# Grouped logits issued two pairs at a time over all eight PSUM banks, in a four-layer cross-attention kernel

## The chip, the cores and the metric

The kernel runs on one NeuronCore of one Trainium2 chip. The metric is device microseconds of one execution: the median of three runs before the change is 3410.82 us (3410.70 to 3411.05). Engines are called PE (TensorE matmul), PEld (its weight loads), DVE (VectorE), ACT (ScalarE), POOL (GpSimd) and SP (SyncE, which issues DMAs).

## The reference

Four cross-attention layers run one after the other on a state `x` of 4 batches, 512 queries and 256 channels, all in float32, with a context of 1024 keys and 512 channels. Layers 0, 2 and 3 ("masked") have 16 heads of 64 and add a bias to the logits of a few key columns; layer 1 ("grouped") normalises `x` first and has 16 heads of 16 that share 4 key/value heads:

```python
# masked layers 0, 2, 3
logits = einsum('bhqd,bhkd->bhqk', x @ Wq, ctx @ Wk) * 64 ** -0.5 + col_bias
x = softmax(logits) @ (ctx @ Wv) @ Wo + bo + x
# grouped layer 1
xn = rmsnorm(x, norm_w)
scores = einsum('btgrd,bsgd->bgrts', xn @ wq, ctx @ wk) * 16 ** -0.5
x = x + softmax(scores) @ (ctx @ wv) @ wo
```

The softmax subtracts a maximum before the exponential, so the maximum of the logits is computed too.

## The kernel before, in words

**Units and steps.** A unit is a pair of heads of a masked layer, or four heads' worth of a grouped layer (`u` from 0 to 7 in each layer and batch; `g.h` is `u % 2`). `order()` writes out by hand which masked unit `g` and which grouped unit go together. The main loop runs over these steps. In a step, `g` is the masked unit whose logits are made, `g1` the masked unit of the step before, which is attended, `lam` the grouped unit that is attended, and `coming` the grouped unit of the next step, whose logits are made already now. There are 32 steps with a `coming`; in 28 of them there is also a `lam` (in the first of each batch there is none).

**One step on PE**, in order: `scores(g)` (L873, with two bfloat16 bias matmuls, L879), `attend(g1)` (L906), then a list `fill` of pieces of projections: the queries of the next unit (L770), output projections (L1112), and either the keys of the next two masked units (`k_part`, L556: a "key step") or the values of two (`v_pair`, L609: a "value step"). Two successive pieces of keys or of values fill one PSUM bank, which ACT copies out (L561, L616) after the second. After roughly 9.5 us of fill by a hand-written estimate (8.0 in value steps) come the sums of `g1` (L1078) and `attend_grouped` (L906 with 128x32 tiles), and from 12 us on the four calls of `logits_pair` for `coming` (L846), spread between the remaining fill pieces by due times.

**A pair** is two tiles of 128 keys by 1024 (two heads by 512 queries). It is eight PE instructions in tiles of 32 rows, four of which run at once. Each tile takes two PSUM banks. ACT copies it to SBUF (L852), DVE takes its block maxima (`block_max`, L930), and after the last of eight tiles `max_quarters` and `max_everywhere` (L946 to L970) make the maximum of the unit. In the next step POOL subtracts it from the eight tiles (`subtract`, L976), ACT takes the exponentials (L984), and then `attend_grouped` can run.

**After the grouped attention**, `keep_even` (ACT, L916) copies one half of the result from its PSUM bank and `keep_odd` (DVE, L920) adds the other half. For units with `g.h == 1`, which are attended in key steps, `turn_grouped` then normalises through the same bank (DVE, L1033 to L1039).

**PSUM.** `Place` hands out the 8 banks: two-bank places go to even pairs, one-bank places in these steps to banks 4 to 7, the longest free first. The matmul that takes a bank waits for whoever read it last. All orders on the engines are those in which the program issues; there is no other scheduler.

Of the kernel before, what the change touches and what calls it, by code (L numbers as in the profile page):

```python
# [17 lines left out]
B, S, C = 4, 512, 256  # L18
# [62 lines left out]
def kernel(ctx: ExitStack, tc: tile.TileContext, a: dict, out: bass.AP):  # L81
# [17 lines left out]
    returns = [0]  # L99

    tabled = [False]

    class Place:
        def __init__(self, width=2, last=2, among=(4, 5, 6, 7)):
            free = given_back
            if width == 2:
                whole = [n for n in range(0, 8, 2) if n in free and n + 1 in free]
                if tabled[0]:
                    whole = [n for n in whole if n <= last] or whole
                at = min(whole, key=lambda n: max(free[n], free[n + 1]))  # L110
            elif tabled[0] and any(n in free for n in among):
                at = min((n for n in among if n in free), key=lambda n: free[n])
            else:
                at = min(free, key=lambda n: free[n] + (2 if n ^ 1 in free else 0))
            self.banks = range(at, at + width)
            for n in self.banks:
                del free[n]
            self.ap = ps_all[:, at : at + width, :].rearrange("p n q -> p (n q)")
# [642 lines left out]
    def project_q(g):  # L761
        if g.n in first_queries:
            g.qt = x_all[:, g.n // 2, g.n % 2, :]
        else:
            g.qt = t_([P, S], "qt", f"qt_{g.name}", bufs=2)
        x = xs[g.l, g.b]
        w = Place(1)
        m = w.ap
        for k in range(KC):
            nc.tensor.matmul(m, lhsT=g.wq[:, k, :], rhs=x[:, k, :], start=(k == 0), stop=(k == KC - 1))  # L770
        if g.last:
            drop_state(g.l, g.b)

        def evacuate():
            nc.scalar.mul(g.qt, m, 0.125)
            w.back()

        return evacuate
# [59 lines left out]
        return evacuate  # L838


    def logits_pair(g, i):
        ws = [Place(), Place()]
        for odd in range(2):
            for j in range(2):
                rows = slice(64 * odd + 32 * j, 64 * odd + 32 * (j + 1))
                nc.tensor.matmul(  # L846
                    ws[odd].ap[:, j * S : (j + 1) * S], lhsT=g.kt[rows, i * P : (i + 1) * P],
                    rhs=g.qt[rows, :], start=True, stop=True,
                )
        for odd, w in enumerate(ws):  # L850
            t = 2 * i + odd
            nc.scalar.copy(g.st[t], w.ap)  # L852
            if tabled[0]:
                w.back()
                block_max(g, t)
            elif t == 0:
                g.mx_place = w
            else:
                w.back()
                top = g.mx_place.ap  # L860
                nc.vector.tensor_tensor(top, top, g.st[t], ALU.max)
# [56 lines left out]
    def keep_odd(g):  # L918
        half = gq[g.b, "o"][64 * g.h : 64 * (g.h + 1), :]
        nc.vector.tensor_tensor(half, half, g.po[64:128, :], ALU.add)  # L920
        if g.h == 0:
            g.place.back()

# [11 lines left out]
    def max_quarters(g):  # L937
        other = t_([64, 32], "other", f"other_max_{g.name}")
        g.every = t_([P, 2 * S // 32, 1], "every", f"every_{g.name}")
        if tabled[0] and g.masked:  # L940
            g.mb_place = w = Place()
        else:
            w = Place(1)
        quarter, half = w.ap[:, 0:32], w.ap[0:64, 32:64]
        if tabled[0]:
            nc.vector.tensor_reduce(quarter, tops.rearrange("p t b -> p b t"), AX.X, ALU.max)  # L946
        else:
            over_quarter(quarter, g.mx_place.ap, ALU.max)
            g.mx_place.back()
        nc.vector.tensor_copy(other, quarter[64:128, :])  # L950
        nc.vector.tensor_tensor(half, quarter[0:64, :], other, ALU.max)
        for h in range(2):
            nc.vector.tensor_copy(
                other[32 * h : 32 * (h + 1), :], half[32 * (1 - h) : 32 * (2 - h), :]
            )
        for h in range(2):
            nc.vector.tensor_tensor(
                g.every[64 * h : 64 * (h + 1), :, 0], half, other, ALU.max
            )
        if not (tabled[0] and g.masked):  # L960
            w.back()
# [61 lines left out]
        nc.gpsimd.tensor_tensor(g.acc, g.st[0] if t == 1 else g.acc, g.st[t], ALU.add)  # L1023

    def turn_grouped(g):
        normalise_grouped(g, g.place.ap)
        g.place.back()

    def normalise_grouped(g, m):

        o = gq[g.b, "o"]
        short = t_([P, S // 32, 1], "short", f"short_{g.name}")
        nc.vector.transpose(m, o)  # L1033
        nc.vector.reciprocal(short, m.rearrange("p (c r) -> p c r", r=32)[:, :, 16:17])
        nc.vector.transpose(
            m.rearrange("p (c r) -> p c r", r=32), short.to_broadcast([P, S // 32, 32])
        )
        g.ot = o
        nc.vector.tensor_tensor(o, o, m, ALU.mult)  # L1039
        if g.u % 4 == 1:  # L1040
            nc.sync.dma_start(out=o_kept, in_=o)
        else:
            for i in range(4):
                nc.sync.dma_start(
                    out=o[32 * i + 16 : 32 * (i + 1), :], in_=o_kept[32 * i : 32 * i + 16, :]
                )
# [241 lines left out]
    for n in range(len(steps) + 2):  # L1288
        g, lam = at(n)
        follows, coming = at(n + 1)  # L1290
# [5 lines left out]
        kk = []  # L1296
# [71 lines left out]
        def pair(i):  # L1368
            if i == 0:
                pass_events(STAY)  # L1370
                while late:
                    late.pop(0)()
                take_set(coming)
            logits_pair(coming, i)
            if by_ones and events:
                events.pop(0)[2]()
            if i == NT // 2 - 1:
                max_quarters(coming)
                max_everywhere(coming)
# [66 lines left out]
        of_queries = []  # L1446
        if follows and follows.n not in first_queries and not comes_late(follows, n):
            of_queries.append((1.7, lambda: project_q(follows)))
        if fast_k:
            of_keys = fast_keys(*kk)  # L1450
            if fresh:
                of_keys[1:4] = of_keys[3:4] + of_keys[1:3]
            fill = of_keys[:2] + fill + of_keys[2:4] + of_queries + of_keys[4:]
        elif fast_v:
            of_values = fast_values(g)
            if fresh:
                of_values[1:4] = of_values[3:4] + of_values[1:3]
                fill = of_values[:2] + fill + of_grouped + of_values[2:4] + of_queries + of_values[4:]
                of_grouped = []
            else:  # L1460
                fill = of_values[:2] + fill + of_queries + of_values[2:]
        else:
            fill += of_queries
            if kk:
                fill += keys(*kk)
        of_values = values(g) if g and g.n % 2 == 0 and not fast_v else []
        before = 2 if by_ones else 4
        fill += of_values[:before] + of_grouped + of_values[before:]
        if lam:

            def attend_grouped():
                while any(of is lam for _, of, _ in events):
                    events.pop(0)[2]()
                lam.v = head(lam).v
                place_out(lam)
                attend(lam)
                give_set(lam)
                late.append(lambda: keep_odd(lam))
                if lam.h == 1:
                    late.append(lambda: turn_grouped(lam))  # L1480
                return lambda: keep_even(lam)

            total, where = 0.0, 0
            while where < len(fill) and total < (8.0 if by_ones and of_values else 9.5):
                total += fill[where][0]
                where += 1
            fill.insert(where, (3.6, attend_grouped))
            if by_ones:
                fill.insert(where, (1.0, lambda: late.insert(0, sums_beside(g1))))
        elif by_ones:  # L1490
            fill.insert(2, (1.0, lambda: late.insert(0, sums_beside(g1))))
# [27 lines left out]
            fill.append((0.9, by_products))  # L1519
        now = 0.0  # L1520
        for us, w in fill:
            while pairs and pairs[0][0] <= now:
                pair(pairs.pop(0)[1])
                now += 1.0
                pairs = [(max(at, now + 1.6), i) for at, i in pairs]
            done = w()
            now += us
            if callable(done):
                pass_events(now)
                done()  # L1530
        while pairs:
            pair(pairs.pop(0)[1])
        behind_exponentials()
        if lam and lam.u % 4 == 3:
            ready.append(lam)
# [32 lines left out]
```

## Time and profile before

| what | value |
|---|---|
| median of three runs | 3410.82 us |
| profiled execution | 3411.3 us, of which span 3409.5 us |
| PE busy | 3396.9 us (100%), 15520 instructions |
| DVE, ACT, POOL busy | 2956.4 us (87%), 2348.4 us (69%), 2596.1 us (76%) |
| granted PE clock | 1.00 |
| L846 (pairs of grouped logits) | 1024 PE instructions, 160.0 us busy |
| L852 (their copies) | 256 on ACT, 1.02 us each |
| L976, L1023 (POOL subtractions, running sums) | 256 of 2.38 us, 668 of 2.37 us |

Of each execution 1.8 us lie outside the span. A PE that is busy all the time is not one that works all the time: ends of matmuls are modelled, and a short wait between two kinds of matmul doesn't show as idle time. Starts are measured, so what a group of matmuls costs is read from its start to the start of the next group.

### The profile page before, as it was taken

How to read it: one execution, taken by the hardware profiler on the slowest of the kernel's cores; microseconds unless marked ns; L12 is line 12 of the kernel's file. 1: busy time of each engine (PE TensorE's matmuls, PEld its weight loads, DVE VectorE, ACT ScalarE, POOL GpSimd, SP SyncE). 2: the span in 40 equal slices, each digit the busy share in tenths (PEclk: the TensorE clock that was granted, in tenths of full speed). 3: DMA queues.
4: the chain of work that ended last, by engine and by line, in shares of the span. 5: the costliest groups of instructions: out<-in, count | busy, mean ns of one | idle time of the engine just before them, and what ended most of it. 6: DMA issues, size and time to landing. Idle time of an engine off the chain costs nothing.

```text
span 3409.5 us, 42702 instructions
## 1 busy us (share of the span) xinstructions
PE 3396.9 (100%) x15520; PEld 1654.2 (49%) x15520; DVE 2956.4 (87%) x3872; ACT 2348.4 (69%) x2729; POOL 2596.1 (76%) x1337
## 2 busy tenths in 40 slices
PE   9999999999999999999999999999999999999999
PEld 5555444444444444445455454554444445454554
DVE  7888899988999889988888889888899988889887
ACT  5666688776787768876666666666678776666665
POOL 5888588875888768888668768677588888769775
PEclk9999999999999999999999999999999999999999
DMA  3232111011101120011001110011111101011100
GB/s 109 64 115 85 58 36 52 30 48 38 55 27 30 48 62 30 27 30 55 19 28 53 35 48 30 28 53 56 38 30 52 36 21 53 28 45 52 35 30 10
DMA packets 147733, 151.69 MB, mean 44 GB/s; under 512 B 23608, under 2 KB 125496, under 8 KB 147012
## 3 DMA queue, kind: packets, MB, share of 16 engines
q1 hardware_dynamic: 144958, 140.58, 13.2%
q0 software_dynamic: 2560, 8.39, 0.9%
q8 instruction: 123, 2.02, 0.3%
q14 instruction: 86, 0.70, 0.1%
q10 hardware_dynamic: 6, 0.00, 0.0%
HBM read 132.15 MB, written 15.73 MB: 43 GB/s over the span
## 4 chain that ended last, share of the span: by engine, by line
PE 92%; DVE 5%; ACT 1%; issue 1%; POOL 0%; DMA 0%; DVEq 0%; ACTq 0%; POOLq 0%
PE ps L906 21%; PE ps L669 18%; PE ps L873 18%; PE ps L556 9%; PE ps L609 9%; PE ps L1112 5%; PE ps L770 5%; PE ps L846 4%; DVE ps L890 2%; DVE st L978 1%; PE ps L1078 1%; PE ps L571 1%; ACT st L883 1%; PE ps L879 1%; PE ps L785 0%
## 5 line engine op out<-in xcount | busy, mean ns | idle before, releaser
L1023 POOL TENSOR_TENSOR st<-st 128x1024 f32<-128x1024 f32 x668 | 1581.7, 2368 | 557.1 <-ACT st L984 512.6
L984 ACT ACTIVATE st<-st 128x1024 f32<-128x1024 f32 x1024 | 1042.3, 1060 | 226.8 <-POOL st L976 117.7
L978 DVE TENSOR_TENSOR st<-st,ps 128x1024 f32<-128x1024 f32 x768 | 884.2, 1214 | 3.3
L906 PE MATMUL ps<-st,v 128*64 128x512 f32 (+1 forms) x4064 | 789.8, 595 | 0.0
L976 POOL TENSOR_TENSOR st<-st 128x1024 f32<-128x1024 f32 x256 | 597.8, 2379 | 212.0 <-DVE st L970 106.2
L883 ACT COPY st<-ps 128x1024 f32<-128x1024 f32 x768 | 713.3, 1053 | 55.6 <-PE ps L879 55.4
L890 DVE TENSOR_TENSOR ps<-ps,st 128x1024 f32<-128x1024 f32 x420 | 517.8, 1233 | 210.2 <-ACT st L883 172.1
L930 DVE TRANSPOSE_TENSOR_REDUCE tops<-st 128x32 f32<-128x1024 f32 x544 | 628.3, 1211 | 69.2 <-ACT st L852 64.5
L873 PE MATMUL ps<-qt,kt 64*128 64x512 f32 x3008 | 687.3, 596 | 0.0
L906 PEld LDWEIGHTS ps<-st,v 128*64 128x64 f32 (+1 forms) x4064 | 239.9, 130 | 535.0 <-issue 443.6
L873 PEld LDWEIGHTS ps<-qt,kt 64*128 64x128 f32 x3008 | 280.9, 186 | 345.0 <-ACT st L883 147.5
L609 PE MATMUL ps<-wv,ctx 128*128 128x256 f32 x1344 | 312.1, 385 | 1.1 <-ACT ctx L432 1.1
L669 PE MATMUL ps<-st 128*128 128x128 f32 (+1 forms) x1620 | 308.8, 339 | 2.3 <-ACT ps L692 2.1
L556 PE MATMUL ps<-ctx,wk 128*128 128x512 f32 x672 | 310.9, 604 | 0.0
L609 PEld LDWEIGHTS ps<-wv,ctx 128*128 128x128 f32 x1344 | 250.5, 190 | 92.1 <-issue 54.8
L852 ACT COPY st<-ps 128x1024 f32<-128x1024 f32 x256 | 247.0, 1018 | 62.5 <-PE ps L846 59.0
L669 PEld LDWEIGHTS ps<-st 128*128 128x128 f32 x1620 | 214.6, 192 | 94.2 <-issue 86.7
L684 ACT COPY st<-ps 128x512 f32<-128x512 f32 x45 | 26.3, 585 | 339.2 <-PE ps L669 339.2
L556 PEld LDWEIGHTS ps<-ctx,wk 128*128 128x128 f32 x672 | 121.9, 190 | 180.5 <-issue 163.4
L770 PE MATMUL ps<-x,wq 128*128 128x512 f32 x376 | 180.6, 603 | 2.0 <-ACT x L393 1.1
L1112 PE MATMUL ps<-ot,wo 128*128 128x512 f32 x380 | 173.2, 599 | 0.0
L846 PE MATMUL ps<-qt,kt 32*128 32x512 f32 x1024 | 160.0, 640 | 0.0
(202 smaller groups left out, 2961.6 us busy)
## 6 DMA issues: line engine op xcount, KB each, us to landing
wv<-in_L_xattn_Wv_dram SPq DMA_DIRECT2D x48, 512.0 KB
ctx<-kept SPq DMA_DIRECT2D x24, 1024.0 KB
wk<-in_L_xattn_Wk_dram SPq DMA_DIRECT2D x47, 512.0 KB
wo<-in_L_xattn_Wo_dram SPq DMA_DIRECT2D x96, 128.0 KB
wq<-in_L_xattn_Wq_dram SPq DMA_DIRECT2D x94, 128.0 KB
st<-kept SPq DMA_DIRECT2D x4, 2048.0 KB
qt<-q SPq DMA_DIRECT2D x64, 128.0 KB
kept<-st SPq DMA_DIRECT2D x12, 512.0 KB
```

The source lines that it names most:

```text
L556: nc.tensor.matmul(m, lhsT=g.w["k"][:, k, :], rhs=ctx_half[g.b, n][:, k, :], start=(k == 0), stop=(k == KT - 1),)
L609: nc.tensor.matmul(m[:, half * 2 * P : (half + 1) * 2 * P], lhsT=ctx_half[g.b, t // 4][:, k, t % 4 * P : (t % 4 + 1) * P], rhs=g.w["v2"][: ...
L669: nc.tensor.matmul(m if is_keys else m[:, q], lhsT=right[:, k, :] if is_keys else left_[:, k, q], rhs=left_[:, k, :] if is_keys else right ...
L873: nc.tensor.matmul(m[:, j * S : (j + 1) * S], lhsT=g.kt[g.rows[j], keys], rhs=g.qt[g.rows[j], :], start=True, stop=t > 0,)
L883: nc.scalar.copy(g.st[t], m)
L890: nc.vector.tensor_tensor(top, top, g.st[t], ALU.max)
L906: nc.tensor.matmul(g.po[at, :], lhsT=g.v[:, t, rows], rhs=g.st[t][:, j * S : (j + 1) * S], start=(t == first), stop=(t == last),)
L930: nc.vector.tensor_reduce(out_, of.rearrange("p (b x) -> p b x", x=32), AX.X, op, apply_transpose=True)
L976: nc.gpsimd.tensor_tensor(g.st[t], g.st[t], g.mb, ALU.subtract)
L978: nc.vector.tensor_tensor(g.st[t], g.st[t], g.mb, ALU.subtract)
L984: nc.scalar.activation(st, st, AF.Exp)
L1023: nc.gpsimd.tensor_tensor(g.acc, g.st[0] if t == 1 else g.acc, g.st[t], ALU.add)
```

## The change: what it does

In steps that have both a `lam` and a `coming`, the four pairs are no longer spread by due times. Two of them are put directly after the grouped attention, then two pieces of keys or values, then the other two, then the rest. The eight tiles get fixed banks: the pairs use (0,1)+(2,3), (4,5)+(6,7), (2,3)+(4,5), (6,7)+(0,1). The pieces after each double pair are sent to banks 0 and 2 (`hinted`). So that a bank's two pieces stay together, the grouped attention moves one piece later where an odd number of them had come before it. `turn_grouped` works in SBUF (`g.mx`), and the bank of the grouped attention is given back right after `keep_odd`. `max_quarters` of a grouped unit uses bank 7. The one masked exponential that waits among the pairs comes after the second pair instead of the first.

```diff
-        def __init__(self, width=2, last=2, among=(4, 5, 6, 7)):
+        def __init__(self, width=2, last=2, among=(4, 5, 6, 7), at=None):
             free = given_back
-            if width == 2:
+            if at is not None or width == 1 and hinted:
+                at = hinted.pop(0) if at is None else at
+            elif width == 2:
...
-    def logits_pair(g, i):
-        ws = [Place(), Place()]
+    PAIR_BANKS = ((0, 2), (4, 6), (2, 4), (6, 0))
+
+    def logits_pair(g, i, fixed):
+        ws = [Place(at=PAIR_BANKS[i][odd] if fixed else None) for odd in range(2)]
...
         nc.vector.tensor_tensor(half, half, g.po[64:128, :], ALU.add)
-        if g.h == 0:
-            g.place.back()
+        g.place.back()
...
-            w = Place(1)
+            w = Place(1, among=(7,))
...
     def turn_grouped(g):
-        normalise_grouped(g, g.place.ap)
-        g.place.back()
+        normalise_grouped(g, g.mx[:, 0:S])
...
-            logits_pair(coming, i)
-            if by_ones and events:
+            logits_pair(coming, i, bool(lam))
+            if by_ones and events and i == (1 if lam else 0):
                 events.pop(0)[2]()
...
-            while where < len(fill) and total < (8.0 if by_ones and of_values else 9.5):
+            enough = 8.0 if coming and of_values else 9.5
+            while where < len(fill) and total < enough:
                 total += fill[where][0]
                 where += 1
+            if coming:
+                where += sum(each in of_values + of_keys for each in fill[:where]) % 2
+
+                def two_pairs(bank):
+                    hinted.clear()
+                    pair(pairs.pop(0)[1])
+                    pair(pairs.pop(0)[1])
+                    hinted.extend(range(bank, bank + 2))
+
+                fill.insert(where + 2, (2.0, lambda: two_pairs(2)))
+                fill.insert(where, (2.0, lambda: two_pairs(0)))
             fill.insert(where, (3.6, attend_grouped))
...
-            while pairs and pairs[0][0] <= now:
+            while pairs and not lam and pairs[0][0] <= now:
```

## The prediction

> **What bounds the kernel now.** I read the page first, then the timelines of PE, ACT, DVE and POOL over two neighbouring steps (a key step whose first pair starts at 906.73 and a value step whose first pair starts at 948.57), then the instructions of single lines. Busy times and the chain that ended last:
>
> ```profile
> PE 3396.9 (100%) x15520; PEld 1654.2 (49%) x15520; DVE 2956.4 (87%) x3872; ACT 2348.4 (69%) x2729; POOL 2596.1 (76%) x1337
> ...
> PE 92%; DVE 5%; ACT 1%; issue 1%; POOL 0%; DMA 0%; DVEq 0%; ACTq 0%; POOLq 0%
> ```
>
> PE sets the end everywhere, so only what changes the distance between starts on PE counts. PE's timeline of the key step:
>
> ```profile
> 903.16 3.64 PE L906 MATMUL ps<-st,v 128*32 128x512 f32 x32
> 906.73 1.14 PE L846 MATMUL ps<-qt,kt 32*128 32x512 f32 x8
> 907.80 1.99 PE L556 MATMUL ps<-ctx,wk 128*128 128x512 f32 x4
> 909.72 1.34 PE L846 MATMUL ps<-qt,kt 32*128 32x512 f32 x8
> 910.99 1.98 PE L556 MATMUL ps<-ctx,wk 128*128 128x512 f32 x4
> 912.90 1.41 PE L846 MATMUL ps<-qt,kt 32*128 32x512 f32 x8
> 914.25 1.98 PE L556 MATMUL ps<-ctx,wk 128*128 128x512 f32 x4
> 916.16 1.14 PE L846 MATMUL ps<-qt,kt 32*128 32x512 f32 x8
> 917.23 3.70 PE L556 MATMUL ps<-ctx,wk 128*128 128x512 f32 x8
> 920.86 1.13 PE L873 MATMUL ps<-qt,kt 64*128 64x512 f32 x4
> ```
>
> Four key matmuls take 1.92 us from start to start (907.80 to 909.72), eight take 3.63 (917.23 to 920.86): four more cost 1.71, 0.43 each, so each group pays 0.21 for coming after another tile shape. A pair is two rounds of 0.43 and takes 1.07: again 0.21. The second and third pair take 1.27 and 1.35, 0.20 and 0.28 more; they wait for a bank. And what follows the grouped attention off PE, in the value step, from ACT's, DVE's and POOL's timelines:
>
> ```profile
> 924.22 18.69 POOL L976 TENSOR_TENSOR st<-st 128x1024 f32<-128x1024 f32 x8 [6.28 <-DVE st L970]
> ```
> ```profile
> 938.25 2.01 ACT L984 ACTIVATE st<-st 128x1024 f32<-128x1024 f32 x2 [0.47 <-POOL st L976]
> 940.60 2.00 ACT L984 ACTIVATE st<-st 128x1024 f32<-128x1024 f32 x2 [0.34 <-POOL st L976]
> 942.51 0.57 ACT L616 COPY v<-ps 128x512 f32<-128x512 f32 x1
> 942.97 3.90 ACT L984 ACTIVATE st<-st 128x1024 f32<-128x1024 f32 x4
> 946.77 0.57 ACT L616 COPY v<-ps 128x512 f32<-128x512 f32 x1
> 947.24 2.01 ACT L984 ACTIVATE st<-st 128x1024 f32<-128x1024 f32 x2
> 949.14 0.57 ACT L916 COPY o<-ps 64x512 f32<-64x512 f32 x1
> 949.78 1.93 ACT L852 COPY st<-ps 128x1024 f32<-128x1024 f32 x2
> ```
> ```profile
> 949.74 0.69 DVE L920 TENSOR_TENSOR o<-o,ps 64x512 f32<-64x512 f32 x1 [1.74 <-ACT o L916]
> ```
>
> Read the brackets: from 940.60 ACT is never idle, and it began there because POOL's subtraction had just come. So keep_even (L916, 949.14) comes 24.92 after POOL's first subtraction, by a queue and not by PE, whose attention ended at 948.57. The list of who waited for keep_odd (L920) is empty today. That is what the change alters.
>
> **The gain.** G is the start of a step's first pair. A key step takes 14.13 from G to the next scores; one key piece (1.71) moves ahead of G, so 12.42 is to be compared. New, without waits: two double pairs of 1.07 + 0.86 = 1.93 and two fills of 3.63, 11.12: 1.30 saved (two switches to pairs and two back, 0.84, and 0.48 of bank waits, rounded). A value step takes 12.37 (948.57 to 960.94) and would take 2 x 1.93 + 2 x 3.65 = 11.16: 1.21 saved. All 28 steps would give 28 x 1.26 = 35 us.
>
> **New wait 1: bank 7.** The built program of the changed kernel puts the grouped attention in bank 7 in all these steps, and the last matmul of the second pair, which writes bank 7, waits for keep_odd. keep_even starts 0.14 after G when ACT is free (0.57 in the value step above), takes 0.58, keep_odd follows 0.03 later and takes 0.69: 1.30 in all. Semaphore to matmul takes 0.05 (an L852 copy ends at 909.88, the pair's second half starts at 909.93). Today a half that starts at 909.94 lets the next group begin at 910.99: 1.05. So the double pair lasts (keep_even's delay after G) + 1.30 + 0.05 + 1.05 = delay + 2.40; with a delay of 0.14 that is 2.54 instead of 1.93. Behind that wait stand the fill, the second double pair and the next scores.
>
> **New wait 2: bank 2.** The fill after the second double pair goes to bank 2, which holds that double pair's first tile. Its copy starts 1.23 after the pairs do (917.39 after 916.16) and takes 1.01; with 0.05 the fill starts at 2.29, not 1.93: 0.36 lost in every step. The first fill's bank 0 has the same wait, hidden under wait 1. The two pieces of the first fill lie in bank 0, which the fourth pair needs 0.96 after its double pair starts; their copy ends 0.69 after (916.27 + 0.58 against 916.16): no loss. The exponential moved behind the second pair goes 4.9 to 5.9 after G, in front of that copy at 6.3: nothing, but if keep_even came over 2 us late it would delay it.
>
> **New wait 3: the loop.** keep_even's delay is itself changed. In a key step DVE ends the last block maximum 14.07 after G today (920.81). New: keep_odd ends at 1.44, turn_grouped (2.5, taken unchanged in SBUF) at 3.98, eight maxima at 1.13 end at 13.06; by copies, the second double pair starts at 2.54 + 3.63 = 6.17, its first copy ends at 8.41 and four maxima follow to 13.06. Both say 13.06. Then 3.41 to POOL's first subtraction (920.81 to 924.22) and 24.92 to keep_even: 41.39 after the key step's G. PE meanwhile needs 2.54 + 3.63 + 2.29 + 3.63 = 12.09 to the scores and 27.71 from there to the value step's G (920.86 to 948.57): 39.80. keep_even is 1.59 late instead of 0.57, since the later G of the key step anchors the maxima later, and PE's way is shorter. The next key step is safe. With D for the length of the value step's first double pair, its maxima end at D + 3.65 + 6.89, POOL starts 3.41 later, and keep_even is ready 25.05 (990.86 after 965.82) and one more key copy (0.57) after that, at D + 39.57; PE gets to the next G at D + 3.65 + 2.29 + 3.65 + 29.37 (960.94 to 990.31) + 1.71 = D + 40.67. So its delay is 0.14. turn_grouped's DMA on SP moves with keep_odd, but its readers come in later steps.
>
> **The sum.** New step = delay + 2.40 + fill + 2.29 + fill.
> - 12 key steps: 0.14 + 2.40 + 3.63 + 2.29 + 3.63 = 12.09 against 12.42: -0.33 each, -4.0.
> - 4 first value steps, delay 0.14 (ACT is ready 0.4 before G today and no changed pairs precede): 12.13 against 12.37: -0.24, -1.0.
> - 4 third value steps, which hold an output projection more and also move a piece: 14.17 - 1.72 = 12.45 against 12.13: -0.32, -1.3. Their keep_even is ready within 0.1 of being late.
> - 6 other value steps, delay 1.59: 13.58 against 12.37: +1.21, +7.3.
> - 2 value steps behind a key step that is 0.87 longer (eight transposes; 42.70 instead of 41.83 from G to G): delay 0.72, 12.71: +0.34, +0.7.
>
> Together +1.7 us. On the profiled execution (span 3409.5, 1.8 outside) that is 3413.0; on the median 3410.82 it is 3412.5. Steps without pairs issue the same PE stream. What the traces can't show: the cost of turn_grouped between SBUF operands (by L811 and L1092, 0.69 to 0.71 each; at most 0.1 either way, and the copies hold DVE at 13.06 anyhow); of a fourth row group waiting alone (bounds 0.86, two bare rounds, to 1.07, a pair; I take 1.05): 28 x -0.19 to +0.02, -5 to +1 us; the loop's 24.92 (24.92 to 25.05 in all late steps, 8 x 0.13: +1); wait 2 at 0 to 0.4: -10 to +1.
>
> [...] The row says that the tiles' copies keep up: four follow each other every 0.91 us, 3.65 for a double pair, while PE has over 5.5. [...] The granted clock is 1.00 throughout, and the longest new gap on PE would be about 2.1 us. [...]
>
> **The rivals.** (a) The waits bite less, the switches count: if keep_odd came before the second pair and bank 2 were free, 35 us less, 3376; with wait 1 alone, 28 x (1.26 - 0.61) = 18 less, 3393. For it: the switches are measured. Against: keep_odd's end is measured in 28 steps at 1.44 or later. (b) The loop takes hold in all value steps: if POOL's start slips by over 0.1 in third steps and by more in first ones, these eight also get delays near 1.6 and cost +1.2 instead of -0.3: 8 x 1.5 = 12 more, 3425. It decides from a keep_even later than 0.4 after G there. For it: the third steps' margin is 0.1 us. Against: first value steps follow an unchanged step.
>
> **How the numbers follow.** A measurement of this kernel can tell about 0.2% (6.8 us) from no change. Forecast (no more than that): 0.62, with a range of its own of 3406 to 3417. Rival (a), faster by more: 0.15. Rival (b) or a longer loop, slower by more: 0.23. The range takes the forecast's, the bounds of wait 2 and half of (b): 3402 to 3420.
>
> **What would show it.** In the changed profile: pair groups of 16 PE instructions, the first lasting about 2.54 in key steps and 4.0 in most value steps, the second 2.29; keep_odd as releaser of PE's pair line; keep_even 1.6 after G in the second and fourth value steps. Wrong, if the first group lasts 1.93, if value-step keep_even stays at 0.57, or if the scores stage (7.28 today) grows.

## The result, and the profile after

The changed kernel takes 3433.26 us (median, 3429.86 to 3438.36); the kernel before, run beside it on the same chip, takes 3410.76. The ratio is 1.0067, 95% interval 1.0052 to 1.0082: slower by 22.5 us, outside the range on record. The profiled execution is the quickest one, 3429.86 us with a span of 3427.7, 18.2 more than before's 3409.5. Its mean granted clock is 0.997 where before's was 1.00.

Two lines of the page of the changed kernel. They are all but those of before, except that the chain that ended last now runs more through DVE, ACT and POOL:

```profile
PE 3393.3 (99%) x15520; PEld 1668.2 (49%) x15520; DVE 2959.4 (86%) x3872; ACT 2345.6 (68%) x2729; POOL 2600.8 (76%) x1337
...
PE 86%; DVE 8%; ACT 3%; POOL 2%; issue 1%; DMA 0%; DVEq 0%; ACTq 0%; POOLq 0%
```

PE's timeline of the changed kernel over the same two neighbouring steps as in the prediction, a key step and the value step behind it (start, busy time, line, idle time before and what ended it; new line numbers: pairs L851, keys L559, values L612, scores L878):

```profile
911.58 2.61 PE L851 MATMUL ps<-qt,kt 32*128 32x512 f32 x16
914.12 3.70 PE L559 MATMUL ps<-ctx,wk 128*128 128x512 f32 x8
917.75 2.00 PE L851 MATMUL ps<-qt,kt 32*128 32x512 f32 x16
920.05 3.70 PE L559 MATMUL ps<-ctx,wk 128*128 128x512 f32 x8 [0.29 <-ACT st L857]
923.68 1.13 PE L878 MATMUL ps<-qt,kt 64*128 64x512 f32 x4
...
951.38 2.32 PE L851 MATMUL ps<-qt,kt 32*128 32x512 f32 x14
955.04 1.12 PE L851 MATMUL ps<-qt,kt 32*128 32x512 f32 x2 [1.34 <-DVE o L925]
956.09 5.38 PE L612 MATMUL ps<-wv,ctx 128*128 128x256 f32 x16
```

The key step is the predicted one to the hundredth: from start to start 2.54, 3.63, 2.30, 3.63, together 12.10 (12.09 was forecast). The value step is not. Its first double pair takes 4.71 (951.38 to 956.09) where 4.0 was forecast, and then sixteen value matmuls take 5.31 where the same fill took 3.65 in 12 of the 16 value steps. So there are two things to explain: 0.7 us in front of the bank 7 wait, and 1.66 us in a fill that waits for nothing. (Value steps are counted within each batch, first to fourth; this is a second one.)

**The late maxima.** DVE's timeline of the key step: keep_odd (L925), `turn_grouped` (to L1042), the eight block maxima (L934):

```profile
912.33 0.69 DVE L925 TENSOR_TENSOR o<-o,ps 64x512 f32<-64x512 f32 x1 [1.73 <-ACT o L921]
...
914.90 1.38 DVE L1042 TENSOR_TENSOR o<-o,st 128x512 f32<-128x512 f32 x1
916.20 9.12 DVE L934 TRANSPOSE_TENSOR_REDUCE tops<-st 128x32 f32<-128x1024 f32 x8
```

The multiplication at the end of `turn_grouped` takes 1.38 us where the prediction had 0.69, and the maxima follow without a gap, so they end 13.74 after G (925.32), not 13.06. From POOL's first subtraction to keep_even it is 24.91 to 24.96 in the second to fourth value steps, as forecast; so the 0.68 arrives whole, and keep_even starts 2.27 to 2.32 after G in six of the second and fourth value steps instead of 1.59, and 1.76 and 1.40 after it in the two behind a longer key step instead of 0.72. In the third value steps, whose margin was 0.1, it starts at 0.55, and their double pair takes 2.98 instead of 2.54.

What ran on POOL at that time (the changed kernel's POOL timeline, two windows; the first row is two running sums of 2.36, the second of which ends at 915.73):

```profile
910.93 4.80 POOL L1027 TENSOR_TENSOR st<-st 128x1024 f32<-128x1024 f32 x2
```
```profile
915.81 2.69 POOL L1027 TENSOR_TENSOR st<-st 128x1024 f32<-128x1024 f32 x1
```

The multiplication, begun at 914.90, ends at 916.28, 0.55 after that POOL instruction does. The same holds in all twelve long ones of this run: they end 0.55 after the POOL instruction in flight, to within 0.02. The four of 0.69 began when POOL had only 0.11 to 0.14 us to go. And the POOL instruction that comes while the multiplication runs takes 2.68 to 2.71 instead of 2.36. The kernel before has the same multiplication with one input in PSUM, and there POOL made no difference to it (minimum, median, maximum in ns):

```profile
L1039 DVE TENSOR_TENSOR o<-o,ps x16: 686/687/689, 494.1 to 2784.1; 128x512 f32<-128x512 f32 x16
```

Four of these sixteen began with 1.49 to 1.51 us of a POOL instruction left, and took 0.69 like the others.

**The slow fill.** Busy time by stretch, the double pair and the fill behind it (length, then PE, PEld, DVE, ACT, POOL, and the granted PE clock third from the end):

```profile
951.38:956.09 4.71, 3.37 (x21) 1.30 (x17) 2.68 (x4) 4.71 (x8) 4.55 (x3) 1.00 0.00 0
956.09:961.40 5.31, 5.31 (x18) 4.15 (x17) 3.74 (x4) 2.76 (x3) 5.15 (x3) 0.68 0.01 3
```

The clock is halved in part of the fill (the granted clock is 0.50 from 956.09 to 959.00 and 1.00 from 960.00 on), right behind a double pair in which PE was idle for 1.34 and then ran one tile of 32 rows alone for 1.1 (a lone row group; the fill's tiles have 128). Four such stretches lie in the profiled run, three of 3.41 us and one of 6.83, each behind one of the eight long waits of second and fourth value steps. Summed over the fills, and over the one double pair that fell into the longest stretch, against the same pieces at full clock, they cost 1.66 + 1.69 + 1.60 + 3.3 = 8.25 us.

The account of the 18.2 us:

| term | us |
|---|---|
| the prediction's own sum | 1.7 |
| 6 second and fourth value steps, double pair 4.70 not 3.99 | 4.3 |
| 2 behind a longer key step, 4.16 and 3.80 not 3.12 | 1.7 |
| 4 third value steps, 2.98 not 2.54 | 1.8 |
| granted clock halved four times | 8.25 |
| not accounted for | 0.45 |

The executions scatter over 8.5 us while the kernel before stays within 1 or 2; their mean granted clock falls from 0.997 in the two quickest to 0.995 in the slowest.

### The profile page after: what moved, and what is told of

It reads as the page before. It is cut to its first block, busy times and chain, and to the rows that moved or that the text cites. A ratio compares the mean times of both kernels' runs of the same rounds, so it can differ in the third digit from the quotient of the medians.

```text
span 3427.7 us, 42679 instructions
## 1 busy us (share of the span) xinstructions
PE 3393.3 (99%) x15520; PEld 1668.2 (49%) x15520; DVE 2959.4 (86%) x3872; ACT 2345.6 (68%) x2729; POOL 2600.8 (76%) x1337
## 4 chain that ended last, share of the span: by engine, by line
PE 86%; DVE 8%; ACT 3%; POOL 2%; issue 1%; DMA 0%; DVEq 0%; ACTq 0%; POOLq 0%
PE ps L911 20%; PE ps L672 18%; PE ps L878 17%; PE ps L612 8%; PE ps L559 8%; PE ps L1115 4%; PE ps L773 4%; PE ps L851 3%; DVE ps L895 2%; POOL st L980 2%; DVE st L982 2%; ACT st L988 1%; DVE tops L934 1%; PE ps L1081 1%; PE ps L574 1%
## 5 line engine op out<-in xcount | busy, mean ns | idle before, releaser
L878 PE MATMUL ps<-qt,kt 64*128 64x512 f32 x3008 | 687.2, 596 | 0.0
L934 DVE TRANSPOSE_TENSOR_REDUCE tops<-st 128x32 f32<-128x1024 f32 x544 | 622.7, 1206 | 63.4 <-ACT st L857 58.9
L878 PEld LDWEIGHTS ps<-qt,kt 64*128 64x128 f32 x3008 | 280.4, 186 | 345.5 <-ACT st L888 147.6
L612 PE MATMUL ps<-wv,ctx 128*128 128x256 f32 x1344 | 311.2, 388 | 5.8 <-ACT st L857 4.7
L559 PE MATMUL ps<-ctx,wk 128*128 128x512 f32 x672 | 304.3, 600 | 3.5 <-ACT st L857 3.5
L612 PEld LDWEIGHTS ps<-wv,ctx 128*128 128x128 f32 x1344 | 258.0, 194 | 78.8 <-ACT st L857 30.7
L559 PEld LDWEIGHTS ps<-ctx,wk 128*128 128x128 f32 x672 | 123.6, 190 | 178.2 <-issue 148.8
L851 PE MATMUL ps<-qt,kt 32*128 32x512 f32 x1024 | 154.3, 622 | 12.9 <-DVE o L925 12.9
```

Source lines behind the costliest of these rows:

```text
L559: nc.tensor.matmul(m, lhsT=g.w["k"][:, k, :], rhs=ctx_half[g.b, n][:, k, :], start=(k == 0), stop=(k == KT - 1),)
L612: nc.tensor.matmul(m[:, half * 2 * P : (half + 1) * 2 * P], lhsT=ctx_half[g.b, t // 4][:, k, t % 4 * P : (t % 4 + 1) * P], rhs=g.w["v2"][: ...
L878: nc.tensor.matmul(m[:, j * S : (j + 1) * S], lhsT=g.kt[g.rows[j], keys], rhs=g.qt[g.rows[j], :], start=True, stop=t > 0,)
L934: nc.vector.tensor_reduce(out_, of.rearrange("p (b x) -> p b x", x=32), AX.X, op, apply_transpose=True)
```

## The experiments

**Turn in SBUF alone.** The kernel before with two edits of the change: the turn in SBUF, the bank back early.

```diff
-        if g.h == 0:
-            g.place.back()
+        g.place.back()
...
-        normalise_grouped(g, g.place.ap)
-        g.place.back()
+        normalise_grouped(g, g.mx[:, 0:S])
```

> The kernel before with one part of the change alone: turn_grouped works in SBUF, the bank goes back after keep_odd. Theory 1 (the slow multiplication feeds a loop that only the pairing exposes): the multiplication of turn_grouped takes about 1.38 us instead of 0.69, key steps end their block maxima up to 0.7 later, keep_even of the second and fourth value steps comes at about 1.2 after the first pair instead of 0.57, and since no matmul waits for keep_odd here the time stays at 3410.8 within 1.5 us, clock 1.00. Theory 2 (SBUF operands cost nothing by themselves, the long multiplication only appears together with the pairs): 0.69 us, keep_even unchanged, time unchanged. Should the time rise by over 4 us, both are wrong about what waits for DVE.

Measured: 3411.34 us, ratio 1.0002 (0.9992 to 1.0011). No difference in time, but neither theory holds as it stands: the multiplication is long in four of its sixteen runs only. In the other twelve it falls just at the end of a POOL instruction (0.14 to 0.16 us to go). The line's own answer (minimum, median, maximum in ns), in this kernel and in the changed one:

```profile
L1037 DVE TENSOR_TENSOR o<-o,st x16: 691/698/2049, 493.8 to 2784.1; 128x512 f32<-128x512 f32 x16
```
```profile
L1042 DVE TENSOR_TENSOR o<-o,st x16: 691/1372/1729, 494.6 to 2800.8; 128x512 f32<-128x512 f32 x16
```

The 2.05 and 2.01 occur in the four third key steps, where 1.46 to 1.50 us of a POOL instruction was left: again 0.55 more. These are the steps in which the kernel before, at nearly the same phase but with one input in PSUM, took 0.69. So in these two kernels the price of the multiplication goes with its two SBUF inputs and its phase against POOL (2.05 with 1.50 left, and 0.69 with 1.51 left where one input was in PSUM), and in the old schedule little of it is passed on: the maxima of these four steps end 0.30 to 0.34 later, keep_even of three of the steps behind them starts 0.20 to 0.26 later, and those last 0.03 to 0.07 longer.

**The gap filled.** The changed kernel, with the first three matmuls of the second pair done three times over (the same values again) in the second and fourth value steps, so that PE works while its fourth matmul waits:

```diff
...
+        quarters = [(odd, j) for odd in range(2) for j in range(2)]
+        if fixed and i == 1 and g.u in (3, 7):
+            quarters = quarters[:3] * 3 + quarters[3:]
+        for odd, j in quarters:
...
```

> The changed kernel, with the first three matmuls of the second pair done three times over in the second and fourth value steps of each batch, while the fourth waits for keep_odd (same results, 8 x 6 more matmuls). Theory 1 (the clock is halved because PE stands still in that wait): granted clock 1.000 in every run, no throttled stretch at these steps, the double pair still about 4.7 us there, time about 3421.5 us (8.3 less than the profiled 3429.9), and the runs agree within 1 us instead of 8.5. Theory 2 (the double pair of 32-row tiles itself counts as low activity): the clock stays at 0.995 to 0.997 and the time at 3430 to 3438.

Measured: 3421.81 us, ratio 1.0031 (1.0019 to 1.0044), all six runs within 0.13 us. The same two stretches in it:

```profile
949.75:954.43 4.68, 4.68 (x33) 2.44 (x29) 2.69 (x4) 4.68 (x8) 4.52 (x3) 1.00 0.00 0
954.43:958.08 3.65, 3.65 (x17) 2.96 (x17) 3.65 (x4) 2.76 (x3) 3.49 (x3) 1.00 0.00 0
```

The wait is as long, PE does more, and the kernel is 8.0 us faster than the changed kernel's profiled execution (11.5 than its median): the fill is back at 3.65. The granted clock is 1.000 in all six runs, although the lone row group behind the wait is still there. So of these two kernels only the one whose PE stands still in the wait ran at a halved clock behind it (in the mean 0.995 to 0.997 in its four executions, 1.000 in the six with the gap filled), and the scatter goes with it (8.5 us and 0.13).

**The multiplication left out**, without and with the gap filled (three matmuls done twice):

```diff
-        nc.vector.tensor_tensor(o, o, m, ALU.mult)
```

> The changed kernel with the last multiplication of turn_grouped left out, so that the grouped layer's result is not divided by its sum. Theory (the multiplication between two SBUF operands, 1.37 us beside a busy POOL, lengthens the loop from a key step to the next value step): block maxima of key steps end at 13.1 or earlier after G instead of 13.74 (0.69 of the 1.37 was in my sum, so 12.4 if the copies do not hold DVE), keep_even of second and fourth value steps 1.6 or less after G instead of 2.3, their first double pair 4.0 or less instead of 4.7, third value steps 2.54 instead of 2.98. That is 8 x 0.7 + 4 x 0.45 = 7.4 us less than the changed kernel; if the shorter standstill no longer halves the granted clock, another 8 us less: about 3414; if it still does, 3418 to 3424. Rival (the late maxima come from something else, the maximum's bank 7 or DVE's queue): double pairs stay at 4.7 and the time within 2 us of 3430.

> As no_multiply, and the first three matmuls of the second pair are done twice in second and fourth value steps, so that PE has work while its last matmul waits. Theory: the clock stays at 1.00, and the time is that of gap_filled less the loop's 7.4 us: 3421.8 - 7.4 = 3414.4. This is what the prediction's sum would have been with the loop as forecast (3412.5), 2 us off. Rival (the multiplication is not the cause): 3421.8 as before.

Measured: 3416.79 us without the filling (3413.32 to 3424.24 over ten runs, whose mean clock goes from 1.000 at the quickest to 0.997 at the slowest; ratio 1.0018, 1.0009 to 1.0028), between the two times expected, and 3414.39 with it, as expected (3413.37 to 3414.97; ratio 1.0007, 0.9998 to 1.0017). Without the multiplication the maxima of key steps end 13.07 after G, keep_even starts 1.60 to 1.64 after G in six of the second and fourth value steps (1.59 was forecast) and 0.74 to 0.75 in the two behind a longer key step (0.72), and 0.14 in the third. The value step that was 4.71 and 5.31 (PE's timeline, multiplication left out, gap not filled):

```profile
948.71 1.99 PE L851 MATMUL ps<-qt,kt 32*128 32x512 f32 x14
951.68 1.12 PE L851 MATMUL ps<-qt,kt 32*128 32x512 f32 x2 [0.98 <-DVE o L925]
952.73 3.72 PE L612 MATMUL ps<-wv,ctx 128*128 128x256 f32 x16
```

4.02 and 3.65. With the gap filled as well the kernel stands 2.4 us above the kernel before, and the prediction's sum was +1.7. The two terms are thus the whole of the error but for 0.7 us, which is within the interval. A standstill of 0.97 was still followed by a halved clock once in the profiled run (near 2575: the granted clock is 1.00 from 2570 to 2573.84 and 0.76 in the mean from there to 2581).

**The turn behind the maximum.** The changed kernel with `turn_grouped` moved from in front of the block maxima to behind the chain of the maximum, where it works in another SBUF buffer:

```diff
-        normalise_grouped(g, g.mx[:, 0:S])
+        normalise_grouped(g, st_slot((NT + 1) * min(sets_free) + NT)[:, 0:S])
...
                 max_quarters(coming)
                 max_everywhere(coming)
+                while behind_max:
+                    behind_max.pop(0)()
...
-                    late.append(lambda: turn_grouped(lam))
+                    (behind_max if coming else late).append(lambda: turn_grouped(lam))
```

> The changed kernel, with turn_grouped moved behind the maximum of the coming unit, so that DVE's block maxima no longer stand behind it. Theory 1: maxima end 13.06 after the first pair in key steps instead of 13.74, keep_even of the second and fourth value steps comes at 1.6 instead of 2.29, their first double pair lasts 4.0 instead of 4.7, third value steps 2.55 instead of 2.98: 6 x 0.69 + 2 x 0.69 + 4 x 0.44 = 7.3 us less, so 3422.6 with the clock still halved now and then, 3414 if the shorter standstill no longer halves it. Theory 2 (the delay comes from POOL or ACT queues, not from this multiplication): keep_even stays at 2.2 or later and the time at 3430 to 3438.

Measured: 3445.38 us, ratio 1.0101 (1.0084 to 1.0118). Slower still: the expectation was wrong. The maxima do end at 13.07, but now the turn's 3 us stand in DVE's queue in front of the next step's work. What PE waited for in this kernel (us in total, times, longest):

```profile
PE ps L851 <- DVE ot L812: 11.1, 6, 1.9
PE ps L851 <- DVE o L925: 7.9, 4, 2.0
```

The first line is new. L812 transposes the sums of `g1` out of the bank that the first pair takes; it comes late, and PE cannot even begin the pairs. keep_even is also 26.10 after POOL's subtraction instead of 24.9, and the mean granted clock is 0.996 here too. So DVE has no room behind the maximum either: moving the turn moves the wait.

**Exponentials behind.** The changed kernel, nothing left out, but three masked exponentials (ACT, 0.95 each) held back instead of one: two behind the second pair's copies and one behind the fourth's. This takes 1.9 us out of ACT's queue ahead of keep_even, the queue that the loop runs through:

```diff
-            if by_ones and events and i == (1 if lam else 0):
+            for _ in range(min(len(events), {1: 2, 3: 1}.get(i, 0) if lam else int(by_ones and i == 0))):
                 events.pop(0)[2]()
...
-                stays = by_ones and t > 6
+                stays = by_ones and t > (4 if lam and coming else 6)
```

> The changed kernel, with three masked exponentials (t = 5, 6, 7) instead of one held back: two follow the second pair's copies, one the fourth's. Nothing is left out. Theory 1 (what costs is keep_even standing in ACT's queue behind them): keep_even comes 1.9 us earlier, at 0.4 in the second and fourth value steps, the first double pair lasts 2.8 there and 2.54 elsewhere, no throttled stretch, clock 1.000: about 3404 us, faster than both kernels, runs within 1 us. Theory 2 (the double pairs themselves are slow and lower the clock): double pairs over 4 us or a clock below 1 remain, and the time stays above 3420. If the held-back exponentials delay POOL's sums into the next subtraction, about 3408 to 3412.

Measured: 3405.28 us (3405.14 to 3406.70), ratio 0.9984 (0.9974 to 0.9993): faster than both kernels. keep_even starts 0.16 after G in all 28 steps, the first double pair takes 2.57 to 2.59, and the clock stays at 1.00 (0.999 in one of ten runs). PE's key step, and the multiplication:

```profile
906.20 2.64 PE L851 MATMUL ps<-qt,kt 32*128 32x512 f32 x16
908.77 3.70 PE L559 MATMUL ps<-ctx,wk 128*128 128x512 f32 x8
912.40 2.34 PE L851 MATMUL ps<-qt,kt 32*128 32x512 f32 x16
914.70 3.70 PE L559 MATMUL ps<-ctx,wk 128*128 128x512 f32 x8
```
```profile
L1042 DVE TENSOR_TENSOR o<-o,st x16: 691/692/693, 494.9 to 2776.3; 128x512 f32<-128x512 f32 x16
```

With the exponentials later, POOL's running sums have nothing to add yet: POOL is idle from 907.91 to 912.28, and the multiplication takes 0.69 all sixteen times. Delay and multiplication went together here, so this run does not part the two.

**What the two bank waits cost.** exps_behind with the fourth matmul of the second pair, which writes bank 7, left out (`if fixed and i == 1 and odd and j: continue`):

> exps_behind with the last of the four matmuls of the second pair left out, the one that writes bank 7 and waits for keep_odd; its part of the logits stays what it was. Theory (28 double pairs of 2.57 are bound by that one wait): the first double pair falls to 2.29, then bound by the copy of bank 0 as the second one is, or to 1.9 if that copy is early enough; 28 x 0.28 = 7.6 us less, about 3397.5 (3387 at 1.9). Rival (the pairs are bound by ACT's copies or by the row groups, not by bank 7): 3405 as before, less 28 x 0.05.

Measured: 3405.15 us, ratio 0.9980 (0.9971 to 0.9990). Nothing gained: the number is the rival's, but not for its reason, since the first double pair did fall from 2.57 to 2.29 in 24 of the 28 steps, but there the second rose from 2.29 to 2.52 to 2.55. ACT's timeline of that kernel:

```profile
908.00 3.76 ACT L858 COPY st<-ps 128x1024 f32<-128x1024 f32 x4 [0.49 <-PE ps L852]
911.62 2.03 ACT L989 ACTIVATE st<-st 128x1024 f32<-128x1024 f32 x2
913.52 0.60 ACT L564 COPY kt<-ps 128x512 f32<-128x512 f32 x1
```

From 908.00 on ACT is not idle: four copies, two exponentials, then the copy of the first fill's bank 0 (L564), which the fourth pair needs. That copy ends at 914.12 whatever PE does, so an earlier PE waits there. The two exponentials, harmless behind a 2.57 wait, had no slack left. Two more runs took one of them away from that place (one behind the second pair, two behind the fourth); one again without the bank 7 matmul, one with nothing left out and the copy of the second double pair's first tile made in two halves:

```diff
-            nc.scalar.copy(g.st[t], w.ap)
+            if fixed and t == 4:
+                for j in range(2):
+                    nc.scalar.copy(g.st[t][:, j * S : (j + 1) * S], w.ap[:, j * S : (j + 1) * S])
+            else:
+                nc.scalar.copy(g.st[t], w.ap)
```

> no_bank7 again (last quarter of the second pair left out), with one exponential behind the second pair and two behind the fourth instead of two and one. In no_bank7 the first double pair fell from 2.57 to 2.29 and the second rose from 2.29 to 2.55: its odd half waits for the copy of the first fill's bank 0, which stood behind two exponentials on ACT. With one exponential less there, that copy is ready when PE has done the fill. Theory: both double pairs 2.29, so 28 x 0.27 = 7.5 us less than exps_behind, about 3398. Rival (the waits of a step add up to a fixed time that ACT or DVE sets elsewhere): 3405.

> exps_behind with nothing left out, one exponential behind the second pair and two behind the fourth, and the copy of the second double pair's first tile made as two copies of 128x512, so that bank 2 comes free after the first of them. Theory (wait 2 is the 1.01 us copy of 128x1024): the fill may start 1.23 + 0.57 + 0.05 = 1.85 after the second double pair does, so that this is bound by PE's own 1.93; 28 x 0.36 = 10 us less than exps_behind, about 3395. Rival (the second double pair is bound by the bank 0 copy or by the row groups): 2.29 as before and 3405, or 2.2 with 3403.

Measured: 3398.35 us (ratio 0.9963, 0.9949 to 0.9977) without the bank 7 matmul, as expected: both double pairs take 2.29 in 24 of the 28 steps. Wait 1 costs 7 us in all (24 x 0.28 = 6.7 from the first double pairs; the other stages are as in exps_behind), once the loop and the copy of bank 0 are out of it. With the copy in two: 3401.43 us (ratio 0.9972, 0.9961 to 0.9983), the fastest kernel that leaves nothing out, but 6 us short of its expectation. PE's key step in it:

```profile
910.97 2.00 PE L851 MATMUL ps<-qt,kt 32*128 32x512 f32 x16
912.90 3.70 PE L559 MATMUL ps<-ctx,wk 128*128 128x512 f32 x8
```

The second double pair is at the bare 1.93 in all 28 steps, so wait 2 is the 1.01 us copy, as the prediction had it, and 28 x 0.36 = 10 us came off there. Over 6 were given back: the stage of the next scores grew from 7.28 to 7.47 in the mean (28 x 0.19 = 5.3), and in six second and fourth value steps keep_even starts 0.24 later (1.4). The two exponentials behind the fourth pair stand in front of the copies of these scores, but they are not the reason alone: without the bank 7 matmul they stand at the same place and the stage stays at 7.28. There the second double pair still takes 2.29; here PE comes to the scores 0.36 sooner, while ACT, which is not idle from 912.13 to 927.60 in this key step, has as much to do in front of these copies as there.

## Why the prediction was wrong

- **Pairing and its gain:** right. Groups of 16 instructions; two switches saved, with 12.10 measured in a key step against 12.09. The 35 us of a change without waits no run shows; the fastest, the copy in two and the one without the bank 7 matmul, stayed 9.5 and 12.6 below the kernel before.
- **Wait 1, bank 7:** right in its mechanism and size: 2.54 in key steps and first value steps, keep_odd as releaser, double pair = delay + 2.40 with every delay measured at full clock (2.32 gives 4.72; 4.71 was seen).
- **Wait 2, bank 2:** right: 2.29 in all 28 steps, released by the tile's copy.
- **Wait 3, the loop:** its path was right (24.92 and 3.41 were met), its start was not. The failing step is "turn_grouped between SBUF operands ... at most 0.1 either way, and the copies hold DVE at 13.06 anyhow". The rows that I took for its price, L811 and L1092, were not like it: a transposition has one input, and L1092 reads PSUM for one of its two. The multiplication is the one instruction that the change turns from one SBUF input to two, and it cost 0.67 to 0.70 more in eleven key steps and 1.04 in one while POOL ran. And the cover was none: by the prediction's own working DVE's queue and the copies both came to 13.06, so there was no slack in which the 0.69 could hide. Without the multiplication the end stays at 13.07, since the copies hold it from below. Together 7.8 us.
- **What the price should have been.** In all twelve long cases the multiplication ends 0.55 after the POOL instruction that was in flight: it took 1.38 with 0.83 of POOL's instruction left, 2.05 with 1.50 left (turn in SBUF alone), and 0.69 with 0.14 left; with one input in PSUM it took 0.69 with 1.51 left. No row of the kernel before shows such an instruction with two SBUF inputs beside POOL's running sums, so nothing there bounded it at 0.1. An estimate from these runs is 0.69 beside an idle POOL up to 2.37 + 0.55 = 2.92 behind a whole running sum of POOL, and that is the bound that should stand in place of 0.1.
- **The granted clock:** wrong. The step said that it is 1.00 throughout, with a longest new gap of about 2.1 us; that it stays at 1.00 across such a gap was the author's estimate, and the kernel before does not show it (the longest wait of PE there is 1.1 us). The measurement decides against it: the runs show stretches at a granted clock of 0.50 behind 1.11 to 1.34 us of idle PE, beginning 0.46 to 1.16 after the lone row group did, and one behind 0.97 of idle PE. The forecast gap was not even reached: in a double pair of 4.0 PE is idle for 0.97, and the lone row group takes the next 1.05. The halved clock took 8.25 us of the profiled execution, and the multiplication had a hand in it, since it made the waits longer (without it the profiled execution has one halved stretch and not four).
- **The rivals:** (b) was the nearest, slower through the loop. Its mechanism, a start of POOL later by over 0.1 in the third value steps, did occur, at 0.45 a step; first value steps, which it also needed, kept their delay of 0.14. It gave 3425, and the changed kernel with its gap filled took 3421.8, but that nearness is luck: six of the 7.8 us come from second and fourth value steps, where (b) had nothing to add.

Which of the eight long waits of the changed kernel were followed by a halved clock can be read from its trace:

| double pair from | value step | PE idle in it, us | granted clock behind it |
|---|---|---|---|
| 531.96 | second | 1.11 | 0.50 from 536.23 for 3.41 |
| 951.38 | second | 1.34 | 0.50 from 956.07 for 3.41 |
| 1371.34 | second | 1.31 | 0.50 from 1375.91 for 3.41 |
| 2580.13 | second | 1.32 | 0.50 from 2584.23 for 6.83 |
| 703.50 | fourth | 1.32 | 1.00 |
| 1123.43 | fourth | 1.33 | 1.00 |
| 1543.33 | fourth | 1.34 | 1.00 |
| 2754.71 | fourth | 0.76 | 1.00 |

Idle time alone does not part them: 1.11 us was followed by a halved clock, 1.34 was not. In this trace the four stretches start 419.84, 419.84 and 1208.32 us apart, which is 123, 123 and 354 times the 3.413 of the short ones. What else decides whether the clock is halved behind a wait no run shows, and with one trace of each kernel it is not shown either why the executions of one kernel differ.

What stays open is 0.45 us of the account.

## What to carry to other kernels

When two ways to the same instant come out equal, neither hides anything: price what stands on each as if it lay bare. When an operand moves from PSUM to SBUF, look at what the neighbour engine does in that microsecond and not only at the duration of the nearest row: here 0.69 us became 1.38 beside POOL's running sums. And a wait that makes the matmul engine stand still costs its own length and, as here, can be followed by a halved clock (8.25 us of the profiled execution); work put into the gap, even useless work, took 8.0 us off here, and with the shift of a queue elsewhere the granted clock was 1.000 in nine of ten executions.

## What the runs showed of the hardware

- A DVE `tensor_tensor` of 128x512 float32 with both inputs in SBUF took 0.69 us beside an idle POOL and 0.69 to 2.05 beside POOL's running sums: in the twelve long cases of the changed kernel the rest of the sum in flight, plus 0.55, and 0.69 where only 0.11 to 0.14 was left. The running sum behind it took 2.68 to 2.71 instead of 2.36. With one input in PSUM it took 0.69 at both phases that occurred (0.17 to 0.20 and 1.49 to 1.51 us of the POOL instruction left).
- The granted PE clock was 0.50 for 3.41 us at a time, or 6.83, behind four of the eight standstills of 0.76 to 1.34 us of the changed kernel, each of them ahead of a lone row group that took 1.05 to 1.10 (1.58 where the clock was already halved in it), and once behind a standstill of 0.97 in the kernel without the multiplication. The mean granted clock differed between executions of one kernel: over ten runs of one of them the time went from 3413.32 at clock 1.000 to 3424.24 at 0.997.
- Doing three matmuls three times over in a wait made the kernel 8 us faster than the best of its four executions without them.
